# ScalarE fetches 64 columns of x a group in place of 60, VectorE 32 in place of 36, and the batch statistics of the ring stand ahead of the scores

## The chip, the cores and the metric

The kernel runs on one core of a Trainium2 chip. The metric is device time in microseconds for one execution. The core has five engines with an instruction stream each: TensorE (PE in the profile, its weight loads PEld), VectorE (DVE), ScalarE (ACT), GpSimd (POOL) and SyncE (SP). They run side by side and wait for one another on semaphores; SP and POOL issue nearly all of the DMAs here.

## The reference

One graph-attention layer with a residual, a batch normalization, a second residual and a layer normalization, all in float32. x has 12500 nodes of 128 features. There are 212500 edges, sorted by their target `dst`, each with a 128-feature `edge_attr`. Cut to what matters:

```python
Q, K, V = x @ WQ, x @ WK, x @ WV              # per node, 8 heads of 16
Eh = edge_attr @ WE                           # per edge
score = K[src] * Q[dst] / sqrt(16) * Eh
score = exp(clip(score.sum(-1), -5, 5))       # one number per edge and head
wV = segment_sum(V[src] * score, dst)
Z  = segment_sum(score, dst)
h = x + wV / (Z + 1e-6)
gnn = batchnorm(h, over the nodes) * gamma + beta
out = layernorm(x + gnn)
```

## The kernel before, in words

Edges are packed 128 to a tile, 1661 tiles in all. Four tiles that share a window of 64 target nodes form a unit, two units a group: 8 tiles, 1024 edges, 208 groups (the last one has 5 tiles). In the first 100 us or so the kernel loads x transposed into SBUF (`hx`, 128 features x 12500 nodes, resident for the whole run) and writes a table `kvd` with K and V of each node to HBM. Then it goes over the groups.

For every tile the K and V rows of its 128 source nodes have to come into a slot in SBUF. A slot holds the 8 tiles of one group, and there are nine slots. Three ways lead into it:

- **By an indirect DMA** from `kvd`, which GpSimd issues (`gather`, line 303), one for each tile. This is the common way.
- **By columns of x.** The eighth tile of most groups is not gathered. Instead ScalarE (`fetch_cols`, line 409) or VectorE (`fetch_v`, line 395) copies 128 columns of `hx`, one source node each, into a 128x128 tile (`xc` or `xv`), one instruction to a column. TensorE multiplies the full tile by the K and V weights (`cols_mm`), and ScalarE copies the product into the slot (`cols_out`, line 451). The position of a column is a register value, loaded in batches of at most 12 by a TENSOR_LOAD (`load_cols` and `load_v`, both through line 373) from the id tables `col_ids` and `v_ids`. ScalarE fetches COLS columns in a group, VectorE V_COLS, from group 8 on until the lists are used up.
- **By rows**: SP copies the rows of `kvd` one at a time (line 427), 16 in a group, and ScalarE puts them into the slot (line 437).

Functions `col_plan`, `row_plan` and `v_plan` choose at build time which groups take their eighth tile in one of the last two ways: 91 groups by ScalarE's columns, 55 by VectorE's, 24 by rows, 170 in all. The other groups gather all 8 tiles.

What one group does, by engine: TensorE makes Eh (`ps_e`, line 812) and Q per edge by a one-hot matrix (`ps_q`, line 821). VectorE multiplies both into the K part of the slot (`products`, line 837, four instructions), sums by head (`scores`, line 844), clips (line 853), makes the one-hot matrices (lines 778 and 785), finishes the attention of an earlier group (lines 889 to 896) and forms the messages (line 859). ScalarE takes the exponentials (lines 854 and 855) between the clip and the message. TensorE sums the messages by target (`gather_sum`, line 880). ScalarE copies windows and sums about (lines 766, 799, 885) and writes the new rows h into a ring of 1024 columns in SBUF (`x_out`, lines 925 and 926).

When a chunk of 512 columns of the ring is complete, `bn_parts` does two things for it: VectorE takes its mean and variance (`bn_part`, BN_STATS, line 929), and SP stores the chunk to `hT` in HBM (line 550) and then fills the place with the chunk of x that comes two later (`fill_ring`, line 546). There are 23 such refills. A refill waits for the store and for the statistics, and the `x_out` that writes into the refilled place waits for the refill.

The order on every engine is the order in which the loop at the end of the function is written (manual schedule). A gather is put into GpSimd's stream when a slot comes free after `message`; `pace` ties each gather to a VectorE or ScalarE step of the current group, so that it isn't issued earlier than that step. Behind the groups come the last statistics, the second residual and the layer normalization.

Of the kernel before, what the change touches and what calls it, by code (L numbers as in the profile page):

```python
# [33 lines left out]
RING = 1024  # L34
MARGIN = 64
PAD = 2 * MARGIN + WN
COLS = 60
LOAD = 12
V_LOAD = 12
ROOM = 16  # L40
PITCH = 80
FIRST_COL = 8
COL_LAG = 3
EXP_AT = 2
# [2 lines left out]
FIRST_ROW = 8  # L47
ROW_LAG = 2
NSEM = 6
V_COLS = 36  # L50
V_PITCH = 48
HX = 18688
RX = 80480


LAST = [3, 2]
# [23 lines left out]
def wraps(low, high):  # L80
    return high + WN > (low // RING + 1) * RING


def col_plan(sizes):
    full = sizes.count(U) // 2
    groups, end = [], P
    while FIRST_COL + -(-end // COLS) - 1 + COL_LAG < full:
        groups.append(max(NX, FIRST_COL + -(-end // COLS) - 1 + COL_LAG))
        end += P
# [4 lines left out]
def row_plan(sizes):  # L94
    full, used = sizes.count(U) // 2, set(col_plan(sizes))
    groups, end = [], P
    while True:
        g = FIRST_ROW + -(-end // SP_ROWS) + ROW_LAG
        while g in used:
            g += 1  # L100
        if g >= full:
            return groups
        used.add(g)
        groups.append(g)
        end += P


def v_plan(sizes):
    full, used = sizes.count(U) // 2, set(col_plan(sizes) + row_plan(sizes))
    tiles, at, end = [], [], P  # L110
    while True:
        m = FIRST_COL + -(-end // V_COLS)
        while (m - FIRST_COL) * COLS % P < COLS:
            m += 1
# [16 lines left out]
def gnn_kernel(  # L131
# [84 lines left out]
    nc.sync.dma_start(w_kv[:, P:], wv)  # L216
    col_ids = consts.tile([P, 2 * PITCH], I32, name="col_ids")
    v_ids = consts.tile([P, 2 * V_PITCH], I32, name="v_ids")
# [110 lines left out]
    tot = len(col_tiles) * P  # L329
    assert -(-tot // (2 * COLS)) <= P and LOAD <= ROOM and V_LOAD <= ROOM  # L330
    row_tiles = row_plan(usizes)
# [26 lines left out]
    def load_col_ids():  # L358
        load_ids(col_ids, COLS, 0, tot, LOAD)
        load_ids(row_ids, SP_ROWS, tot, tot_rows)  # L360
        load_ids(v_ids, V_COLS, tot + tot_rows, tot_v, V_LOAD)

    def addresses():
        nc.vector.tensor_scalar(row_ids, row_ids, 8 * P, None, op0=OP.mult)
        for ids in (col_ids, v_ids):
            nc.vector.tensor_scalar(ids, ids, 4, HX, op0=OP.mult, op1=OP.add)

    def whole_words(at, start, last):
        return at.with_bounds(min_val=start, max_val=start + 4 * last, guaranteed_mod_val=0, out_of_modulus=4)

    def load_at(engine, ids, q, pitch, k, n, of):
        at, n = q % 2 * pitch + k * ROOM, min(of, n - k * of)
        _, offs = nc.values_load_multi_w_load_instructions(  # L373
            ids[q // 2:q // 2 + 1, at:at + n], engines=(engine,), min_val=HX,
            max_val=HX + 4 * (N - 1), skip_runtime_bounds_check_because="node ids")
        return [o.with_bounds(min_val=HX, max_val=HX + 4 * (N - 1), guaranteed_mod_val=0, out_of_modulus=4)
                for o in offs]

    def column(at):
        return hx8[:, ds(at - HX, 4)].bitcast(F32)  # L380

    OFFV = {}

    def load_v(g, k):
        q = g - FIRST_COL
        if 0 <= q < -(-tot_v // V_COLS):
            OFFV[g, k] = load_at(ET.DVE, v_ids, q, V_PITCH, k, V_COLS, V_LOAD)

    def fetch_v(g, k, a=0, n=V_LOAD):
        offs = OFFV.get((g, k), ())[a:a + n]  # L390
        for r, off in zip(range((g - FIRST_COL) * V_COLS + k * V_LOAD + a, tot_v), offs):
            t = r // P
            if t not in XV:
                XV[t] = wp.tile([P, P], F32, name="xv", bufs=2)
            nc.vector.tensor_copy(XV[t][:, r % P:r % P + 1], column(off))  # L395
# [3 lines left out]
    def load_cols(g, k):  # L399
        q = g - FIRST_COL  # L400
        if 0 <= q < -(-tot // COLS):
            OFFS[g, k] = load_at(ET.Activation, col_ids, q, PITCH, k, COLS, LOAD)

# [149 lines left out]
    def locate_ring():  # L553
# [11 lines left out]
        nc.vector.tensor_tensor(ring_i, at, by, op=OP.subtract)  # L565
        nc.vector.tensor_scalar(ring_i, ring_i, 4, RX, op0=OP.mult, op1=OP.add)
        nc.vector.tensor_tensor(at, at, base_f[0:1, :], op=OP.not_equal)
# [3 lines left out]
    def locate():  # L571


        nc.vector.tensor_copy(base_f, base_i)
        nc.vector.tensor_scalar(base_at, base_i[0:1, :], 4, HX, op0=OP.mult, op1=OP.add)
        nc.vector.tensor_sub(lim[:, :NW - 1], base_f[:, 1:], base_f[:, :NW - 1])
# [333 lines left out]
    def x_out(g):  # L910
        if g not in AT_RING:
            n = 2 if g % 2 == 0 and g + 1 < NG else 1
            _, at = nc.values_load_multi_w_load_instructions(
                ring_i[0:1, 2 * g:2 * (g + n)], engines=(ET.Activation,), min_val=RX,
                max_val=RX + 4 * (2 * PAD + RING - WN), skip_runtime_bounds_check_because="clipped")
            at = [whole_words(a, RX, 2 * PAD + RING - WN) for a in at]
            for k in range(n):
                AT_RING[g + k] = at[2 * k:2 * k + 2]
        for h in (0, 1):
            w, at, new = 2 * g + h, AT_RING[g][h], NEW[g][:, h * WN:(h + 1) * WN]  # L920
            if wraps(low[w], high[w]):
                at = whole_words(nc.s_assert_within(at, RX, RX + 4 * (2 * PAD - WN),
                                                    skip_runtime_bounds_check_because="clipped"),
                                 RX, 2 * PAD - WN)
                nc.scalar.activation(ring8[:, 4 * RING:][:, ds(at - RX, 4 * WN)].bitcast(F32), new, AF.Copy)
            nc.scalar.activation(ring8[:, ds(at - RX, 4 * WN)].bitcast(F32), new, AF.Copy)  # L926

    def bn_part(j):
        nc.vector.bn_stats(stats[:, j, :], in_ring(cuts[j], cuts[j + 1] - cuts[j]))
        done.add(j)  # L930
# [87 lines left out]
    def bn_parts(a, b):  # L1018
        for w in range(a, b):
            for j in due.get(w, []):  # L1020
                bn_part(j)
                keep_h(j)
# [31 lines left out]
    for g in range(NG - 2):  # L1054
        within(load_rel, g + 3)
        if (g + 6) % RQ == 0 and (g + 6) // RQ in quads:
            load_quad((g + 6) // RQ)
        fetch_rows(g)
        if g % 2:
            load((g - 1) // 2 + 2)  # L1060
        within(products, g)
        load_v(g, 2)
        fetch_v(g, 0, 0, 2)
        within(scores, g)
        load_v(g, 1)
        fetch_v(g, 0, 2, 2)
        for k in range(EXP_AT):
            fetch_cols(g, k)
            load_cols(g, k + 1)
        within(clip_exp, g)  # L1070
        within(turned_onehot, g + 2)
        if g >= 2:
            denom(g - 2)
            fetch_v(g, 0, 4, 4)
            recip(g - 2)
            fetch_v(g, 0, 8, 4)
            attn(g - 2)
        fetch_v(g, 1)
        bn_parts(2 * g - 9, 2 * g - 7)
        place_step(store_places)  # L1080
        late_x = g + 1 < nxg and g + 1 not in SLOT
        if late_x:
            turn_x(g + 1, 0, True)
            turn_x(g + 1, 4, True)
            project_main(g + 1)
        within(eh_mm, g + 1)
        within(qe_mm, g + 1)
        cols_mm(g)
        paced = g >= LATE + 4
        if not paced:  # L1090
            issue()
        else:
            issue(G)
        within(onehot, g + 1)
        if paced:
            for step in (SENT[g - 1], PARTS[g][0], PARTS[g][1], PARTS[g][2], PARTS[g][4], BY["at", g - 2],
                         BY["one", g + 1], BY["exp", g]):
                pace(step)
        within(message, g)
        load_v(g + 1, 0)  # L1100
        for k in range(EXP_AT, -(-COLS // LOAD)):
            fetch_cols(g, k)
            if (k + 1) * LOAD < COLS:
                load_cols(g, k + 1)
            else:
                load_cols(g + 1, 0)
            if k == WINDOW_AT:
                within(q_window, g + 4)
        cols_out(g)
        rows_out(g)  # L1110
        fetch_v(g, 2)
        within(add_x, g - 3)
        within(q_mm, g + 3)
        within(gather_sum, g - 1)
        within(x_out, g - 3)
        within(q_out, g + 3)
        within(sums_out, g - 1)
        if g == 2:
            load_last()
            addresses()  # L1120
        if g % (RUN // 2) == 2 and g > 2 and (g // (RUN // 2) + 1) * SEC < T:
            load_section(g // (RUN // 2) + 1)
        for i, r in enumerate(runs):
            if i and g == placed[i]:
                place(r, placing)
        place_step(turn_places)
        within_checks(g)
        while free and todo and todo[0] in done and not pending:
            load_x()
        if g == NG - 3:  # L1130
            assert done >= set(range(NPRE))
            norm_first()
        if g == LATE - 1:
            tps.close()
            late.append(tps.enter_context(tc.tile_pool(name="late", bufs=1)))
        if g == LATE - 2:
            free.append(NSLOT)
            load_kv()
    last = NG - 1
    g = last - 1  # L1140
# [337 lines left out]
```

## Time and profile before

| what | value |
|---|---|
| median of 3 runs | 1971.6 us (1966.8 to 1976.07) |
| profiled execution, its own time | 1971.08 us |
| its span in the trace | 1969.3 us |
| VectorE busy | 1848.2 us, 94% |
| PE busy, weight loads | 1555.6 us (79%), 1288.4 us (65%) |
| ScalarE busy | 1532.7 us, 78% |
| GpSimd busy | 1449.3 us, 74% |
| line 395, VectorE's columns | 7040 copies |
| line 409, ScalarE's columns | 11648 copies |
| line 303, gathers from kvd | 1427 |

Busy time of an engine counts what it executes, not the loads of registers, waits and branches. A row of the page's fifth part names the line, the engine, the operation, what is written from what, the count, then busy time, the mean of one in nanoseconds and the idle time just before, with what ended it. In the timeline the start and the length of an instruction stand first, and instructions that overlap are merged with their count; on ScalarE and VectorE a short instruction begins before the one ahead of it has ended, so that the time of many is the distance of their starts and not the sum of their lengths.

### The profile page before, as it was taken

The page shows a single profiled execution, that of the slowest core. Times are in us where ns is not written, and L with a number is a line of the kernel's source. Part 1 is how long each engine was busy: PE and PEld are TensorE (multiplying, and loading weights), DVE is VectorE, ACT ScalarE, POOL GpSimd, SP SyncE. Part 2 cuts the span into 40 slices and gives each one's busy share as a digit, 9 for nine tenths or more (in the row PEclk, how much of TensorE's full clock was granted, in tenths as well). Part 3 has the DMA queues.
Part 4 walks back from the last instruction along what each step waited for, and adds up shares of the span by engine and source line. Part 5 has one row for each costly group of instructions (what it writes and reads, how often), then busy time and mean ns, then how long its engine had stood idle before and what let it go on. Part 6 is the DMA issues. An engine that isn't in the chain of part 4 may idle for free.

```text
span 1969.3 us, 64470 instructions
## 1 busy us (share of the span) xinstructions
PE 1555.6 (79%) x13025; PEld 1288.4 (65%) x13025; DVE 1848.2 (94%) x10003; ACT 1532.7 (78%) x13757; POOL 1449.3 (74%) x1527
## 2 busy tenths in 40 slices
PE   7869877778778787778778787787787877877787
PEld 6757666666666666666666666676666666666666
DVE  4458999999999999999999999999999999999997
ACT  2225888798888888888888888888898988888836
POOL 7676777777777777777777777777777777777735
PEclk9889888888898888988888888888898888888899
DMA  7854655665555656555655555655655655565553
GB/s 265 299 167 157 184 189 172 188 189 183 172 184 189 191 185 185 175 180 192 189 187 175 182 183 189 195 181 170 190 180 187 190 183 175 183 188 180 196 188 133
DMA packets 130375, 367.72 MB, mean 187 GB/s; under 512 B 37539, under 2 KB 50510, under 8 KB 116142
## 3 DMA queue, kind: packets, MB, share of 16 engines
q0 software_dynamic: 70544, 191.33, 33.1%
q1 hardware_dynamic: 56236, 171.06, 25.2%
q14 instruction: 305, 2.50, 0.4%
q8 instruction: 104, 1.70, 0.4%
q10 hardware_dynamic: 3186, 1.13, 0.3%
HBM read 337.94 MB, written 25.44 MB: 185 GB/s over the span
## 4 chain that ended last, share of the span: by engine, by line
DVE 63%; issue 10%; DVEq 9%; DMA 7%; PE 5%; ACT 3%; SPq 2%; POOL 1%; ACTq 0%; POOLq 0%
DVE xv L395 19%; DVE msg L859 10%; DVE slot L837 9%; DVEq L373 9%; DVE s L844 9%; DVE oh L778 5%; DVE ot L785 4%; DMA slot<-kvd,srcs 4%; DVE at L896 2%; DVE rz L892 1%; POOL slot L303 1%; SPq L354 1%; PE ps_e L503 1%; PE ps_q L950 1%; DVE s L853 1%
## 5 line engine op out<-in xcount | busy, mean ns | idle before, releaser
L303 POOL DMA_INDIRECT slot<-kvd,srcs x1427 | 1359.3, 953 | 449.2 <-issue 175.1
L409 ACT ACTIVATE xc<-hx 128x1 f32 x11648 | 1143.7, 192 | 31.3 <-DVE oh L778 20.9
L812 PE MATMUL ps_e<-w_e,ea 128*128 128x128 f32 x3322 | 546.7, 328 | 308.3 <-DVE slot L837 306.2
L812 PEld LDWEIGHTS ps_e<-w_e,ea 128*128 128x128 f32 x3322 | 493.2, 233 | 361.2 <-DVE slot L837 348.5
L395 DVE COPY xv<-hx 128x1 f32 x7040 | 516.2, 140 | 6.6 <-issue 5.8
L821 PE MATMUL ps_q<-qs,ot 64*128 64x128 f32 x3322 | 306.7, 323 | 4.6
L880 PE MATMUL ps_a<-msg,oh 128*64 128x136 f32 x3322 | 290.1, 296 | 1.7 <-DVE msg L859 1.7
L821 PEld LDWEIGHTS ps_q<-qs,ot 64*128 64x128 f32 x3322 | 257.8, 223 | 46.2 <-DVE slot L837 17.2
L837 DVE TENSOR_TENSOR slot<-slot,ps_e 128x512 f32<-128x512 f32 x410 | 260.9, 675 | 9.1 <-ACT xw L766 7.9
L837 DVE TENSOR_TENSOR slot<-slot,ps_q 128x512 f32<-128x512 f32 x410 | 261.1, 676 | 1.0 <-PE ps_q L821 0.7
L844 DVE TENSOR_REDUCE s<-slot 128x64 f32<-128x1024 f32 (+1 forms) x208 | 249.8, 1202 | 0.9 <-DVE xv L395 0.3
L859 DVE TENSOR_TENSOR msg<-slot,ps_m 128x1024 f32<-128x1024 f32 (+2 forms) x209 | 247.4, 1185 | 1.6 <-ACT ps_m L854 1.1
L880 PEld LDWEIGHTS ps_a<-msg,oh 128*64 128x64 f32 x3322 | 182.7, 138 | 77.7 <-issue 51.4
L926 ACT ACTIVATE ring<-ps_a 128x64 f32 x408 | 90.9, 223 | 95.5 <-DMA ring<-xT 45.6
L854 ACT ACTIVATE ps_m<-s 128x64 f32<-128x64 f32 (+1 forms) x209 | 47.6, 228 | 134.8 <-DVE s L853 128.0
L778 DVE TENSOR_TENSOR oh<-ps_i,rel 128x512 f32<-128x512 f32 x208 | 141.5, 680 | 0.0
L766 ACT ACTIVATE xw<-hx 128x64 f32 x416 | 82.7, 246 | 53.2 <-issue 38.2
L905 PE MATMUL ps_a<-ident,at 128*128 128x128 f32 x408 | 88.0, 298 | 11.0 <-ACT os L885 6.5
L785 DVE TENSOR_SCALAR ot<-rbq,wiota 128x512 f32<-128x512 uint8 x188 | 96.6, 514 | 0.0
L905 PEld LDWEIGHTS ps_a<-ident,at 128*128 128x128 f32 x408 | 74.9, 197 | 30.4 <-ACT os L885 8.6
L795 PE MATMUL ps_a<-w_q,xw 128*128 128x128 f32 x416 | 82.7, 281 | 0.4 <-ACT qs L799 0.4
L877 PE MATMUL ps_a<-msg,oh 128*1 128x136 f32 x416 | 82.0, 278 | 0.0
(191 smaller groups left out, 1535.9 us busy)
## 6 DMA issues: line engine op xcount, KB each, us to landing
ea<-eaT SPq DMA_DIRECT2D x103, 1024.0 KB
byrow<-kvd SPq DMA_DIRECT2D x3072, 1.0 KB
slot<-kvd,srcs POOLq DMA_INDIRECT x1427
rbq<-relT SPq DMA_DIRECT2D x94, 128.0 KB
kvd<-slot SPq DMA_DIRECT2D x12, 512.0 KB
kvd<-t SPq DMA_DIRECT2D x12, 512.0 KB
ring<-xT SPq DMA_DIRECT2D x24, 256.0 KB
hT<-ring SPq DMA_DIRECT2D x23, 256.0 KB
```

Of the source, the lines that this page charges most:

```text
L303: return nc.gpsimd.indirect_dma_start(out=out, out_offset=None, in_=table, in_offset=bass.IndirectOffsetOnAxis(ap=part(SRC, e, 1), axis=0))
L373: _, offs = nc.values_load_multi_w_load_instructions(ids[q // 2:q // 2 + 1, at:at + n], engines=(engine,), min_val=HX, max_val=HX + 4 * (N ...
L395: nc.vector.tensor_copy(XV[t][:, r % P:r % P + 1], column(off))
L409: nc.scalar.activation(XC[t][:, r % P:r % P + 1], column(off), AF.Copy)
L778: by(("one", g), nc.vector.tensor_tensor(one, iota_ps[:, None, :WN].to_broadcast([P, k, WN]), r[:, :, None].to_broadcast([P, k, WN]), op=O ...
L785: by(("ot", g), nc.vector.tensor_scalar(OT[g], RB[g], wiota, None, op0=OP.is_equal))
L812: by(("eh", g), nc.tensor.matmul(t[:, j - a, :], EA[g][:, j, :], w_e, start=True, stop=True))
L821: by(("qe", g), nc.tensor.matmul(QE[g][h][:, j, :], OT[g][r, j * P:(j + 1) * P], QS[g][r], start=True, stop=True))
L837: step = nc.vector.tensor_tensor(kv, kv, of[g][i][:, :b - a, :], op=OP.mult)
L844: step = nc.vector.tensor_reduce(SS[g][:, a:b, :], KV[g](a, b, 0).rearrange("p t (h d) -> p t h d", d=DH), axis=AX.X, op=OP.add)
L859: step = nc.vector.tensor_tensor(MSG[g][:, a:b, :P].rearrange("p t (h d) -> p t h d", d=DH), KV[g](a, b, P).rearrange("p t (h d) -> p t h ...
L880: by(("sum", g), nc.tensor.matmul(AGG[g][h * WN:(h + 1) * WN], OH[g][h * n + j], MSG[g][:, h * n + j, :], start=(j == 0), stop=(j == k - 1)))
```

## The change

The batch of columns that is fetched in one group moves by four from VectorE to ScalarE: COLS 60 becomes 64, V_COLS 36 becomes 32. The pitch of the id tables and the addresses of `hx` and the ring follow. The statistics of a finished chunk, with its store and refill, are asked for ahead of the scores of the group instead of behind the attention of an earlier one.

```diff
-COLS = 60
+COLS = 64
 LOAD = 12
 V_LOAD = 12
 ROOM = 16
-PITCH = 80
+PITCH = 96
...
-V_COLS = 36
+V_COLS = 32
 V_PITCH = 48
-HX = 18688
-RX = 80480
+HX = 18816
+RX = 80608
...
         within(products, g)
         load_v(g, 2)
+        bn_parts(2 * g - 9, 2 * g - 7)
         fetch_v(g, 0, 0, 2)
         within(scores, g)
...
         fetch_v(g, 1)
-        bn_parts(2 * g - 9, 2 * g - 7)
         place_step(store_places)
```

The plan follows from the sizes: 98 groups now take their eighth tile from ScalarE's columns (12544 copies), 48 from VectorE's (6144), 24 by rows: 170 again, so that the gathers from `kvd` stay 1427. ScalarE's columns run over 196 groups (194 before), VectorE's over 192 (195 before). Now 64 is not a multiple of 12, so that ScalarE has a sixth batch of 4 columns with a register load of its own.

The first place is the end of a group on ScalarE, between the window copy (`xw`) and the write into the ring. Before:

```order
L766 ACTIVATE xw<-hx 128x64 x2
L409 ACTIVATE xc<-hx 128x1 x12
L373 TENSOR_LOAD col_ids
L451 ACTIVATE slot_46705<-ps_e 128x256
L913 TENSOR_LOAD ring_i
L926 ACTIVATE ring<-ps_a 128x64 x2
```

Now:

```order
L766 ACTIVATE xw<-hx 128x64 x2
L409 ACTIVATE xc<-hx 128x1 x12
L373 TENSOR_LOAD col_ids
L409 ACTIVATE xc<-hx 128x1 x4
L373 TENSOR_LOAD col_ids
L451 ACTIVATE slot_42476<-ps_e 128x256
L913 TENSOR_LOAD ring_i
L926 ACTIVATE ring<-ps_a 128x64 x2
```

Two rows are new: a register load (of 4 values) and four copies; the load of the next group's first 12 values stands behind them.

The second place is VectorE in a group in which a chunk of the ring is complete. Before, from the last piece of the attention to the message:

```order
L896 SCALAR_TENSOR_TENSOR at<-os,keep,rz 128x128
L395 COPY xv<-hx 128x1 x12
L929 BN_STATS stats<-ring 128x6
L777 TENSOR_TENSOR oh<-rel,lim 128x1
L778 TENSOR_TENSOR oh<-ps_i,rel 128x512
L859 TENSOR_TENSOR msg<-slot_41104,ps_m 128x8x128
```

Now, from the columns at the end of the group before to the clip:

```order
L395 COPY xv<-hx 128x1 x8
L837 TENSOR_TENSOR slot_41182<-slot_41182,ps_e 128x4x128 x2
L837 TENSOR_TENSOR slot_41182<-slot_41182,ps_q 128x4x128 x2
L373 TENSOR_LOAD v_ids
L929 BN_STATS stats<-ring 128x6
L395 COPY xv<-hx 128x1 x2
L844 TENSOR_REDUCE s<-slot_41182 128x64
L373 TENSOR_LOAD v_ids
L395 COPY xv<-hx 128x1 x2
L853 TENSOR_SCALAR s<-s 128x64
```

The statistics stand between the products and the scores, and the last batch of columns in a group has 8 copies where it had 12. In this place BN_STATS waits for ScalarE's writes to the ring by a wait of its own; in the old one an earlier VectorE instruction had waited for a later ScalarE one.

The third place is SP ahead of the fourth group, where the id tables are loaded. Before:

```order
L354 DMA col_ids<-rsrc 97x2x12 x5
L354 DMA col_ids<-rsrc 1x8
L354 DMA row_ids<-rsrc 96x32
L354 DMA v_ids<-rsrc 97x2x12 x3
L354 DMA v_ids<-rsrc 1x12 x4
L354 DMA v_ids<-rsrc 1x8
```

Now:

```order
L354 DMA col_ids<-rsrc 98x2x12 x5
L354 DMA col_ids<-rsrc 98x2x4
L354 DMA row_ids<-rsrc 96x32
L354 DMA v_ids<-rsrc 96x2x12 x2
L354 DMA v_ids<-rsrc 96x2x8
```

One full list transfer more (98x2x4 in place of 1x8), and five transfers of a single row are gone.

## The prediction

> **What bounds the kernel now.** First the page's head, for the shares of the engines.
>
> ```profile
> span 1969.3 us, 64470 instructions
> PE 1555.6 (79%) x13025; PEld 1288.4 (65%) x13025; DVE 1848.2 (94%) x10003; ACT 1532.7 (78%) x13757; POOL 1449.3 (74%) x1527
> ```
>
> VectorE looks like the bound, and GpSimd like an engine with a quarter to spare. The busy times by stretch say otherwise (POOL's columns alone: stretch, length, busy time and count, clock, DMA share, GB/s).
>
> ```profile
> 300.00:500.00 200.00, 151.47 (x160) 0.89 0.59 182
> 900.00:1100.00 200.00, 151.52 (x160) 0.90 0.60 187
> 1500.00:1700.00 200.00, 151.50 (x160) 0.86 0.60 188
> ```
>
> GpSimd issues exactly 160 gathers in each 200 us, one every 1.25 us, and its timeline shows the same 0.30 us between any two. That gap is part of a gather; the only real waits are two early ones. The end of the stream is in the same view.
>
> ```profile
> 163.77 0.95 POOL L303 DMA_INDIRECT slot<-kvd,srcs  x1 [7.49 <-DVE rz L889]
> 184.99 0.94 POOL L303 DMA_INDIRECT slot<-kvd,srcs  x1 [2.71 <-DVE msg L859]
> 1876.68 0.95 POOL L303 DMA_INDIRECT slot<-kvd,srcs  x1 [0.30 <-DMA slot<-kvd,srcs]
> 1885.55 0.95 POOL L303 DMA_INDIRECT slot<-kvd,srcs  x1 [0.30 <-issue]
> 1891.79 0.95 POOL L303 DMA_INDIRECT slot<-kvd,srcs  x1 [0.30 <-issue]
> ```
>
> From 185 to 1893 us GpSimd runs without a stop. So there are two streams, gathers and groups, and the slots between them are the buffer. Which one sets the end? The last group has 5 tiles, so the last five gathers are its own; seven before them (from 1877.93 to 1885.55) belong to the group ahead, and 1876.68 closes the one before that, the third last. The chain of waits has one case in which VectorE did wait for a gather; it shows how long a gather takes to land, counted from its start.
>
> ```profile
> 173.79 2.66 DMA slot<-kvd,srcs
> ```
>
> VectorE's timeline has the products of the last three groups:
>
> ```profile
> 1900.56 1.28 DVE L837 TENSOR_TENSOR slot<-slot,ps_e 128x512 f32<-128x512 f32 x2
> 1911.42 0.68 DVE L837 TENSOR_TENSOR slot<-slot,ps_e 128x512 f32<-128x512 f32 x1
> 1917.20 0.54 DVE L837 TENSOR_TENSOR slot<-slot,ps_e 128x384 f32<-128x384 f32 x1
> ```
>
> The third last group begins at 1900.56 on rows that had landed by 1876.68 + 2.66 = 1879.34: 21.2 us of stock. The second half of the next (1911.42) has 1911.42 - 1888.21 = 23.2, the last one still more. So VectorE's side sets the end, but GpSimd stands 21 us behind it: **whatever the group loop gains beyond 21 us is lost to the gathers**, which this change leaves in number and rate.
>
> Then the groups of one engine in a long steady stretch, 300 to 1800 us, first ScalarE, then VectorE, then GpSimd:
>
> ```profile
> L409 ACT ACTIVATE xc<-hx 128x1 f32 x10290 | 1010.4, 192 | 25.3 <-DVE oh L778 17.9 <-issue 6.7
> L926 ACT ACTIVATE ring<-ps_a 128x64 f32 x344 | 76.6, 223 | 56.9 <-DMA ring<-xT 39.4 <-PE ps_a L880 6.0 <-ACT slot L451 2.5
> L854 ACT ACTIVATE ps_m<-s 128x64 f32<-128x64 f32 x172 | 39.1, 228 | 85.2 <-DVE s L853 81.6 <-DVE xv L395 1.9 <-DVE oh L778 0.5
> L889 DVE TENSOR_SCALAR rz<-os 128x8 f32<-128x8 f32 x171 | 29.5, 172 | 5.4 <-ACT os L885 5.4
> L303 POOL DMA_INDIRECT slot<-kvd,srcs x1193 | 1136.4, 953 | 363.9 <-issue 129.6 <-DVE xv L395 53.7 <-DVE slot L837 50.9
> ```
>
> 172 exponentials in 1500 us are 8.72 us a group. VectorE waits for others for about 7 us in all of it, so its own need is 8.68. ScalarE waits 17.9 + 39.4 + 6.0 + 84.0 = 147 us for others, 0.86 a group; its own need is **7.86 us**. ScalarE has room, but less than the 78% of the page make one think: 0.86 us a group.
>
> **VectorE's term.** Four copies fewer in each group from 8 to 199.
>
> ```profile
> 841.31 0.81 DVE L395 COPY xv<-hx 128x1 f32 x12
> 842.04 1.27 DVE L837 TENSOR_TENSOR slot<-slot,ps_e 128x512 f32<-128x512 f32 x2
> ```
>
> Twelve copies take 842.04 - 841.31 = 0.73 us to the start of what follows, 0.061 each. 7040 - 6144 = 896 copies are 54.7 us, 0.24 a group: 8.68 becomes 8.44. The shorter register load lies under the message and saves nothing.
>
> **ScalarE's term.** Four copies more and one register load.
>
> ```profile
> 916.27 2.33 ACT L409 ACTIVATE xc<-hx 128x1 f32 x24
> 921.34 0.40 ACT L766 ACTIVATE xw<-hx 128x64 f32 x2 [0.23 <-issue]
> 921.65 1.21 ACT L409 ACTIVATE xc<-hx 128x1 f32 x12
> 1794.10 0.40 ACT L766 ACTIVATE xw<-hx 128x64 f32 x2 [0.47 <-issue]
> L373 ACTq TENSOR_LOAD <-col_ids x971: 767/802/1977, 173.9 to 1874.7; - x195
> L758 ACTq TENSOR_LOAD <-base_at x104: 303/311/750, 36.5 to 1881.2; - x104
> ```
>
> 24 copies take 2.33 us and 12 take 1.21, so 12 more take 1.12, 0.093 each, and the load of 12 registers between the two batches (0.80 us) shows no gap: it is hidden under copies already queued. The four copies cost 0.37 us. The new load has 4 registers, as `base_at` has, and should take 0.31. What it exposes has no row; the nearest one is the window copy, ahead of which in every second group two loads follow each other: the gap is 0.23 there, 0.47 at its worst. In the new place four copies stand between the two loads and give 0.37 of cover. Bounds: 0 (all hidden, as under the batches) and 0.47. I take 0.10, nearer the hidden case, since 0.37 of new cover stands against 0.31 of new load. ScalarE's own need becomes 7.86 + 0.47 = 8.33.
>
> Its waits come on top as far as they are not for VectorE's scores: 39.4 for the ring, 17.9 for the place codes behind L778, 6.0 for PE.
>
> **The statistics' term.** They move ahead by the reduce and what follows it. One group of that kind, and SP's waits:
>
> ```profile
> 904.27 0.47 ACT L926 ACTIVATE ring<-ps_a 128x64 f32 x2
> 905.18 1.27 DVE L837 TENSOR_TENSOR slot<-slot,ps_q 128x512 f32<-128x512 f32 x2
> 910.04 0.68 DVE L929 BATCH_NORM_STATS2 stats<-ring 128x6 f32<-128x512 f32 x1
> SPq L546 <- DMA hT<-ring: 97.7, 23, 9.6
> SPq L546 <- DVE stats L929: 28.8, 11, 4.0
> ```
>
> The statistics would start behind the products at 906.4 instead of 910.0, 3.6 us earlier. SP's refill waited last for the statistics 11 times (28.8 us), and for the store 23 times (97.7 us); only the first kind gets earlier, and I take 9 of ScalarE's 39 us at the ring from it. Another 5 go because a ScalarE group that is 0.47 longer reaches the refill later. Bounds: 0 and 28.8. So 25 stay, with 14 of the 17.9 and the 6.0: 45 us in 172 groups, 0.26 each. VectorE's sum is not changed by the move: 26 instructions as before. The new wait for `x_out`, with the scores, clip, exponential and message queued behind it, finds the ring written by 904.74, 1.7 us before it is asked for. It costs something only where ScalarE runs later than that; bounds 0 and, at 0.6 us for each of 24 chunks, 14 us; I take 1.
>
> **The start's term.** The id tables, loaded while VectorE stands still:
>
> ```profile
> 102.41 12.23 SPq L354 DMA_DIRECT2D col_ids<-rsrc  x6
> 115.08 7.73 SPq L354 DMA_DIRECT2D v_ids<-rsrc  x8
> 124.55 0.38 DVE L366 TENSOR_SCALAR v_ids<-v_ids 128x96 int32<-128x96 int32 x1 [5.33 <-DMA v_ids<-rsrc]
> ```
>
> Five full lists and a single row took 12.23 us, about 2.2 a list. One more list is +2.2; of the 7.73 us of v_ids the five single rows are 7.73 - 3 x 2.2 = 1.1, which go. So +1 us (from -1.1 to +2.2), and nothing hides it: GpSimd's two waits at 163.77 and 184.99 are for VectorE's groups behind this point, so both streams start later.
>
> **The sum.** ScalarE's side is the longer of the two now: 8.33 + 0.26 = 8.59 us a group against VectorE's 8.44, and against 8.72 before. That is 0.13 in each of some 192 groups, 25 us. The gathers let 21.2 of it through. With +1 at the start, and 2 for groups that meet the gathers unevenly (a group of 8 gathers takes 10.0 us, one of 7 takes 8.8) and for the statistics' wait, 18 us remain of the profiled execution's 1971.1 us (span 1969.3 and 1.8 around it; the runs' median is 1971.6): **1953 us**.
>
> **A rule on the gathers.** With no column copies at all (110 to 150 us) and with them:
>
> ```profile
> 110.00:150.00 40.00, 30.37 (x32) 0.82 0.52 147
> 200.00:240.00 40.00, 30.43 (x32) 0.88 0.60 184
> ```
>
> 32 gathers in 40 us both times: VectorE's copies do not hold the gathers up. Were they held up by 0.061 us for each copy, 896 fewer would end the stream 55 us earlier and the loop's 25 us would come through whole: 1971 + 1 - 25 = 1947. The Trainium skill has that rule (SBUF — State Buffer, section "SBUF: two separate sides"): a float32 copy from SBUF to SBUF on VectorE locks GpSimd out of the port through which it writes descriptors. The trace does not bear it out for copies of one column, and the case gets 0.05.
>
> **Rivals.** (1) *The register loads come into the open, and ScalarE sets a slower pace.* From an exposed gap of 8.72 - 7.86 - 0.37 - 0.26 = 0.23 us a group on there is no gain left; at 0.35 each group is 0.12 longer, 23 us over 192 groups, 1995 us; at the worst gap seen, 0.47, 2017. For it: the gaps of 0.23 and 0.47 ahead of the window copy; against it: the four copies between. Chance 0.11. (The Trainium skill, DMA: Bandwidth & Descriptors, section "Latency and other measured facts", gives a register load a floor of about 0.6 us. By that the new load outlasts its cover by 0.23, estimated from that page, and the change would gain nothing; the 0.311 of the 4-register load above speaks against it.) (2) *ScalarE takes most of the gain*: an exposed gap of 0.20 leaves 0.03 a group, 6 us, 1966 us. Chance 0.21. (3) *VectorE's 54.7 us come through*: 1917 us. GpSimd's last gather at 1891.79 and ScalarE's 8.33 exclude it; I give 0.01.
>
> **How the numbers follow.** The forecast has 0.62, the freer gathers 0.05. The range holds the forecast's own, from 1947 (no unevenness, an earlier start) up into the second rival at 1968. 0.5%, 10 us, is about what a measurement of this kernel tells from no change. Faster than 1961: forecast, freer gathers, 0.04 of the second rival, 0.72 with the rest; within: 0.17 of the second rival; slower: 0.11.
>
> **What would show it.** Right: the stock ahead of the third last group's products falls from 21 us to a few, VectorE shows waits for gathers late in the run, ScalarE's wait for the scores falls from 81.6 us to a third or less, and GpSimd's last gather stays at 1893 to 1895. Wrong: if the stock is still above 15 us, ScalarE (or the new wait of the statistics) was the bound, and its gaps ahead of L451 and L926 have grown; if the last gather ends elsewhere, the rate or the start was misjudged.

## The result, and the profile after

The changed kernel takes 1952.9 us (median of 5 runs, 1951.1 to 1954.5) against 1973.1 us of the kernel before (5 runs, 1966.8 to 1976.1). The ratio is 0.9899, with a 95% interval from 0.9883 to 0.9915: about 20 us faster, clear of the noise. The profiled execution took 1951.9 us, its span is 1950.1.

The page's head, then the groups of ScalarE from 300 to 1800 us, then two of VectorE and GpSimd's gathers in the same stretch:

```profile
span 1950.1 us, 64649 instructions
PE 1548.8 (79%) x13025; PEld 1279.0 (66%) x13025; DVE 1801.1 (92%) x9107; ACT 1613.6 (83%) x14653; POOL 1454.3 (75%) x1527
```

```profile
L409 ACT ACTIVATE xc<-hx 128x1 f32 x11073 | 1085.7, 193 | 26.0 <-DVE oh L778 16.2 <-issue 7.7 <-DVE msg L859 1.1
L926 ACT ACTIVATE ring<-ps_a 128x64 f32 x346 | 77.3, 223 | 37.6 <-DMA ring<-xT 15.7 <-ACT xc L409 11.3 <-PE ps_e L812 3.6
L766 ACT ACTIVATE xw<-hx 128x64 f32 x346 | 69.7, 248 | 34.8 <-issue 34.6
L451 ACT ACTIVATE slot<-ps_e 128x256 f32<-128x256 f32 x129 | 49.6, 384 | 34.1 <-DMA slot<-kvd,srcs 16.6 <-issue 12.1 <-PE ps_e L812 4.7
L854 ACT ACTIVATE ps_m<-s 128x64 f32<-128x64 f32 x173 | 39.4, 228 | 12.1 <-DVE s L853 5.5 <-DVE xv L395 2.1 <-issue 1.7
L837 DVE TENSOR_TENSOR slot<-slot,ps_e 128x512 f32<-128x512 f32 x346 | 222.8, 681 | 17.9 <-DMA slot<-kvd,srcs 14.1 <-PE ps_e L812 2.6 <-issue 1.0
L929 DVE BATCH_NORM_STATS2 stats<-ring 128x6 f32<-128x512 f32 x21 | 14.5, 693 | 14.6 <-ACT ring L926 14.6
L303 POOL DMA_INDIRECT slot<-kvd,srcs x1191 | 1138.5, 956 | 363.3 <-issue 131.2 <-DVE xv L395 51.2 <-DVE slot L837 36.3
```

ScalarE's wait for the scores (L854 for L853) fell from 81.6 us to 5.5: ScalarE is the longer side of the loop now. VectorE has two waits that it did not have: 14.1 us for gathers, 14.6 for the ring at the statistics. The page's chain of work that ended last shows the same by line. Before:

```profile
DVE xv L395 19%; DVE msg L859 10%; DVE slot L837 9%; DVEq L373 9%; DVE s L844 9%; DVE oh L778 5%; DVE ot L785 4%; DMA slot<-kvd,srcs 4%; DVE at L896 2%; DVE rz L892 1%; POOL slot L303 1%; SPq L354 1%; PE ps_e L503 1%; PE ps_q L950 1%; DVE s L853 1%
```

Now:

```profile
DMA slot<-kvd,srcs 15%; ACT xc L409 13%; DVE xv L395 10%; DVE slot L837 7%; DVE s L844 6%; DVEq L373 4%; DVE ot L785 2%; DVE oh L778 2%; POOL slot L303 2%; DVE msg L859 2%; ACT ring L926 2%; PE ps_e L812 2%; ACTq L373 1%; DVE at L896 1%; PE ps_e L503 1%
```

Landing gathers (`slot<-kvd,srcs`) went from 4% of the span to 15%, and ScalarE's column copies, not listed before, have 13%.

Busy time by stretch shows where the bound changes; VectorE's is the third pair of columns, GpSimd's the fifth:

```profile
600.00:800.00 200.00, 159.85 (x1429) 130.70 (x1429) 199.25 (x1084) 186.26 (x1759) 151.81 (x159) 0.92 0.60 186
1000.00:1200.00 200.00, 158.61 (x1386) 130.14 (x1382) 196.61 (x1060) 182.26 (x1717) 151.55 (x159) 0.89 0.59 186
1400.00:1600.00 200.00, 159.19 (x1356) 129.12 (x1355) 190.02 (x1026) 177.09 (x1660) 151.51 (x159) 0.88 0.59 184
1600.00:1800.00 200.00, 152.34 (x1313) 125.25 (x1311) 189.89 (x1017) 177.37 (x1652) 151.52 (x160) 0.89 0.58 181
```

GpSimd issues 159 or 160 gathers in every stretch, as before. VectorE is nearly full (196.61 of 200 us) as late as 1000 to 1200 us and has some 10 us of air in 200 from 1400 on. In between, at 1280.71, it waits for a gather for the first time in the steady loop:

```profile
1280.71 0.69 DVE L837 TENSOR_TENSOR slot<-slot,ps_e 128x512 f32<-128x512 f32 x1 [1.22 <-DMA slot<-kvd,srcs]
```

There the loop has caught up with the gathers, and from there on it goes at their pace. The exponentials give the pace while stock lasts (200 to 1100 us; count, then the first and the last start). The kernel before:

```profile
L854 ACT ACTIVATE ps_m<-s x103: 221/228/229, 206.5 to 1098.6; 128x64 f32<-128x64 f32 x103
```

The changed kernel:

```profile
L854 ACT ACTIVATE ps_m<-s x105: 226/228/228, 204.9 to 1094.7; 128x64 f32<-128x64 f32 x105
```

That is 892.1 / 102 = 8.75 us a group before and 889.8 / 104 = 8.56 now. The end of both streams in the timeline, GpSimd's and VectorE's:

```profile
1875.36 0.95 POOL L303 DMA_INDIRECT slot<-kvd,srcs  x1 [0.30 <-DVE slot L837]
1890.42 0.95 POOL L303 DMA_INDIRECT slot<-kvd,srcs  x1 [0.30 <-DVE rz L892]
...
1880.87 1.28 DVE L837 TENSOR_TENSOR slot<-slot,ps_e 128x512 f32<-128x512 f32 x2
```

The third last group begins at 1880.87 on rows that had landed by 1875.36 + 2.66 = 1878.02. The stock is 2.9 us, where it was 21.2. The same sum can be made for every group, counted from 0, with the number of gathers that the plan gives each. Before, the stock shrank from 59 us at group 24 to 21 at group 205. In the changed kernel it shrinks from 55 us at group 24 to 2 at group 138 (1279 us) and never exceeds 7 us from there on. From the last gather to the end of the span it was 77.5 us before and is 59.7 now: 17.8 of the 19.2 us by which the profiled spans differ. The other 1.4 are in the gathers, whose last one starts at 1890.42 in place of 1891.79. The last five groups are not set by gathers alone: behind its last wait for one (at 1854.57) VectorE waits 5.2 us for a check of the placed codes, whose matmul (L702) had waited 4.5 us for ScalarE's sums (L885).

```profile
1866.86 0.15 DVE L703 CAST bad_i<-ps_a 1x1 int32<-1x1 f32 x1 [5.18 <-PE ps_a L702]
```

**The start.** Here the trace does not look as forecast. SP's id lists and VectorE's address step after them:

```profile
106.33 5.36 SPq L354 DMA_DIRECT2D col_ids<-rsrc  x6
112.32 1.94 SPq L354 DMA_DIRECT2D v_ids<-rsrc  x3
115.97 0.37 DVE L366 TENSOR_SCALAR v_ids<-v_ids 128x96 int32<-128x96 int32 x1 [1.87 <-DMA v_ids<-rsrc]
167.78 1.28 DVE L837 TENSOR_TENSOR slot<-slot,ps_e 128x512 f32<-128x512 f32 x2
```

A list of 98 rows takes 0.9 us, one of 96 rows 0.65; a list of 97 rows took 2.2. The steady loop starts at 167.78 us, where it started at 176.86, although the lists began 3.9 us later in this execution (106.33, where 102.41), and GpSimd's two waits at 163.77 and 184.99 are gone altogether.

### The profile page after: what moved, and what is told of

It reads as the page before. It is cut to its first block, busy times and chain, and to the rows that moved or that the text cites. A ratio compares the mean times of both kernels' runs of the same rounds, so it can differ in the third digit from the quotient of the medians.

```text
span 1950.1 us, 64649 instructions
## 1 busy us (share of the span) xinstructions
PE 1548.8 (79%) x13025; PEld 1279.0 (66%) x13025; DVE 1801.1 (92%) x9107; ACT 1613.6 (83%) x14653; POOL 1454.3 (75%) x1527
## 4 chain that ended last, share of the span: by engine, by line
DVE 34%; ACT 19%; DMA 19%; issue 11%; PE 7%; DVEq 4%; ACTq 3%; POOL 2%; SPq 0%; POOLq 0%
DMA slot<-kvd,srcs 15%; ACT xc L409 13%; DVE xv L395 10%; DVE slot L837 7%; DVE s L844 6%; DVEq L373 4%; DVE ot L785 2%; DVE oh L778 2%; POOL slot L303 2%; DVE msg L859 2%; ACT ring L926 2%; PE ps_e L812 2%; ACTq L373 1%; DVE at L896 1%; PE ps_e L503 1%
## 5 line engine op out<-in xcount | busy, mean ns | idle before, releaser
L303 POOL DMA_INDIRECT slot<-kvd,srcs x1427 | 1363.5, 956 | 439.8 <-issue 175.3
L409 ACT ACTIVATE xc<-hx 128x1 f32 x12544 | 1229.9, 193 | 32.5 <-DVE oh L778 18.9
L395 DVE COPY xv<-hx 128x1 f32 x6144 | 463.4, 144 | 0.6
L926 ACT ACTIVATE ring<-ps_a 128x64 f32 x408 | 91.2, 224 | 69.1 <-PE ps_a L880 24.1
L766 ACT ACTIVATE xw<-hx 128x64 f32 x416 | 83.4, 248 | 57.2 <-issue 39.8
L451 ACT ACTIVATE slot<-ps_e 128x256 f32<-128x256 f32 x146 | 56.1, 384 | 38.5 <-DMA slot<-kvd,srcs 18.7
```

Source lines behind the costliest of these rows:

```text
L303: return nc.gpsimd.indirect_dma_start(out=out, out_offset=None, in_=table, in_offset=bass.IndirectOffsetOnAxis(ap=part(SRC, e, 1), axis=0))
L409: nc.scalar.activation(XC[t][:, r % P:r % P + 1], column(off), AF.Copy)
```

## The experiments

Eleven of the twelve runs fell on three chips on which the kernel before takes 2866 to 2874 us, and one on a chip on which it takes 1971. What the eleven say is told apart from the one. The changed kernel itself was not run on the three.

### Columns alone

Against the changed kernel:

```diff
         load_v(g, 2)
-        bn_parts(2 * g - 9, 2 * g - 7)
         fetch_v(g, 0, 0, 2)
...
         fetch_v(g, 1)
+        bn_parts(2 * g - 9, 2 * g - 7)
```

> Columns 64 and 32 alone, the statistics in their old place, once more beside the kernel before. If the kernel before takes about 1971 us on this chip: 1953 us, within 2, if the gathers cap the gain (the prediction); up to 1962 if the move of the statistics is a part of it. If it takes some 2870 us again, with ScalarE's instructions at 0.165 us each: 2990 us, since a group then has 5 to 6 instructions more on ScalarE.

This is the run on a chip like the first. It took 1952.1 us (1951.4 to 1954.3) against 1971.3, ratio 0.9901 (0.9879 to 0.9924): the columns, with the lists that they bring, are the whole gain, and the statistics' move adds nothing to it. Its trace says why the move adds nothing; how the gain divides between the columns and the lists it does not show. The exponentials from 200 to 1100 us:

```profile
L854 ACT ACTIVATE ps_m<-s x106: 212/228/229, 201.1 to 1094.2; 128x64 f32<-128x64 f32 x106
```

From 300 to 1800 us, VectorE's products and ScalarE's writes to the ring:

```profile
L837 DVE TENSOR_TENSOR slot<-slot,ps_e 128x512 f32<-128x512 f32 x346 | 222.7, 678 | 31.5 <-DMA slot<-kvd,srcs 28.0 <-issue 3.4
...
L926 ACT ACTIVATE ring<-ps_a 128x64 f32 x346 | 77.3, 223 | 38.5 <-DMA ring<-xT 18.7 <-ACT xc L409 10.0 <-PE ps_e L812 3.1
```

And the last gather:

```profile
1886.67 0.95 POOL L303 DMA_INDIRECT slot<-kvd,srcs  x1 [0.30 <-issue]
```

With the statistics in their old place a group takes 893.1 / 105 = 8.51 us while stock lasts, 0.05 less than in the changed kernel: the move slows the loop a little, since VectorE waits for the ring. What the loop gained by that went into VectorE's wait for gathers, 28.0 us against 14.1 in the same stretch, and the time stayed. That is the cap at work: a loop that is faster by itself ends no earlier. Its first wait for a gather comes at 1186.56, about 94 us before that of the changed kernel:

```profile
1186.56 0.69 DVE L837 TENSOR_TENSOR slot<-slot,ps_e 128x512 f32<-128x512 f32 x1 [1.98 <-DMA slot<-kvd,srcs]
```

The cap is not quite hard at the very end: here the last gather is 3.8 us earlier than in the changed kernel, the third last group begins 2.2 us earlier (1878.70, where 1880.87), the last one 0.9 (1897.16, where 1898.01), and the span is only 0.3 shorter. Behind the last wait for a gather (at 1849.97) VectorE waits 5.2 us for the check of the placed codes, as it does in the changed kernel, so that ScalarE has a part in the last groups of both.

The same kernel ran on one of the other chips too:

> The changed kernel with the statistics in their old place, so columns 64 and 32 alone. If the gathers cap the gain (the prediction), whatever the place of the statistics costs lies in the stock: 1953 us, within 2. If ScalarE's loop sets the end and the move of the statistics is a part of the gain, some 9 us of ScalarE's waits at the ring come back: up to 1962 us.

On that chip it took 2991.0 us against 2872.2: ratio 1.041 (1.039 to 1.044), a loss of 4%.

### What is different on those chips

ScalarE's copies of the columns-alone kernel there, in the timeline, and the group over the whole run:

```profile
1511.85 0.39 ACT L409 ACTIVATE xc<-hx 128x1 f32 x3 [0.30 <-issue]
1512.61 0.20 ACT L409 ACTIVATE xc<-hx 128x1 f32 x1 [0.38 <-issue]
1513.34 0.20 ACT L409 ACTIVATE xc<-hx 128x1 f32 x1 [0.52 <-issue]
...
1514.79 0.20 ACT L409 ACTIVATE xc<-hx 128x1 f32 x1 [0.38 <-issue]
1515.52 0.20 ACT L409 ACTIVATE xc<-hx 128x1 f32 x1 [0.52 <-issue]
1516.23 0.20 ACT L409 ACTIVATE xc<-hx 128x1 f32 x1 [0.51 <-issue]
...
L409 ACT ACTIVATE xc<-hx 128x1 f32 x12544 | 1360.4, 193 | 713.8 <-issue 695.7 <-DMA slot<-kvd,srcs 8.4 <-DVE oh L778 2.8
```

Copies that follow each other every 0.093 us elsewhere start 0.72 us apart for stretches of several us, with nothing that the profile shows them to wait for; the whole run has 696 us of it. VectorE's copies are hardly touched:

```profile
L395 DVE COPY xv<-hx 128x1 f32 x6144 | 466.5, 145 | 11.8 <-issue 11.1
```

In the middle half of the run ScalarE starts one instruction (register loads and semaphores counted) every 0.164 to 0.166 us in the first four kernels, whatever their columns; in the changed kernel on the first chip it is 0.10. VectorE waits 897 us in the columns-alone run there for ScalarE's sums (L889 for L885). So the rate at which ScalarE starts instructions sets the pace there, not the gathers, and a change that gives ScalarE more instructions loses: 118.8 us in 192 groups is 0.62 us for four copies and a register load in each. The granted TensorE clock is lower on these chips too, 0.74 to 0.76 where the first has 0.89; whether that is a cause of the gaps or stands beside them no run separates.

> The kernel of g_after (the changed kernel, 38 gathers replaced by plain loads of 128 rows on SP, so those tiles hold other rows than the reference has), on such a chip: 1927 to 1938 us if the gathers cap the gain, since ScalarE's loop at 8.58 us a group would have ended some 25 us earlier; 1950 to 1955 us if ScalarE's loop sets the end of the changed kernel by itself.

```diff
+    def plain(out, table, e):
+        return nc.sync.dma_start(out=out, in_=table[:P, :])
...
     def pace(step):
+        while queued and queued[0][0] is plain:
+            plain(*queued.pop(0)[1:])
...
-                queued.append((gather, KV[g](j, j + 1, 0, 2 * P).rearrange("p a d -> p (a d)"), kvd,
+                queued.append((plain if j == 0 and g >= 15 and g % 5 == 0 else gather, KV[g](j, j + 1, 0, 2 * P).rearrange("p a d -> p (a d)"), kvd,
```

The rule takes groups 15, 20 and so on to 205, which are 39 and not 38: the traces have 1388 gathers. It ran three times, each time on such a chip: 2921.3, 2931.6 and 2925.6 us, ratios 1.017, 1.022 and 1.018. The two other expectations for it were:

> The changed kernel with 38 of the 1427 gathers (the first tile of every fifth group from 15 on) replaced by one plain load of 128 rows of the table, issued by SP; so those tiles hold other rows than the reference has, and all else stays. GpSimd's stream is 47 us shorter. If the gathers cap the gain (the prediction: ScalarE's own pace of 8.59 us would save 25 us, of which 21 came through; the trace after, with 8.58 us a group while stock lasts, 60 groups short of the end: some 25 us are left over), the time falls to 1927 to 1938 us. If ScalarE's loop sets the end of the changed kernel already: 1950 to 1955. On a chip on which ScalarE's instructions set the pace, no change against the changed kernel, which would be 4% above the kernel before there.

> The kernel of gathers_less once more (the changed kernel with 38 of its 1427 gathers replaced by plain loads of 128 rows on SP). On a chip on which the kernel before takes about 1971 us: the cap theory says 1927 to 1938 us, for the columns alone ran 8.53 us a group while stock lasted and met the gathers some 80 groups before the end; if ScalarE's loop sets the end, 1948 to 1955 us, with VectorE's waits for gathers gone and nothing gained. On a chip on which it takes some 2870 us: 2920 to 2930 us as twice before.

Because the gathers are not the bound there, the cap could not be tested by taking gathers away; on a chip like the first, that was not run. The expectation of the first of the three (g_after) also missed on these chips: I had said no change against some 4%, and the kernel came out 2% above the kernel before. On the same chip, 2931.6 stands against 2996.9 of the changed kernel with other lists (slow_again, below): 65 us, 1.7 us for each gather left out. ScalarE's mean step fell with it, to 0.159 us, and the gaps ahead of its column copies from 699.8 to 621.3 us. In the next kernel they are down to 613.7 us with only six gathers fewer, and that one is the slowest of all, so that what the gaps hang on the runs do not settle.

> The changed kernel with V_COLS 34 in place of 32 and SP_ROWS 18 in place of 16 (the id tables in 98, 96 and 96 rows): VectorE's columns then give 51 tiles and SP's rows 27, six gathers fewer. If the gathers set the end and the loop has 25 us to spare, 6 x 1.25 = 7.5 us less: 1945 us. VectorE's need becomes 8.44 + 0.12 = 8.56 us a group, still not above ScalarE's 8.58. If the loop has no such room, the two columns more come to light, 0.12 x 192 = 23 us: up to 1975 us; if SP falls behind with 18 rows of 0.36 us in 8.7 us, the ring's refills come later and it ends above 1953.

```diff
-SP_ROWS = 16
+SP_ROWS = 18
...
-V_COLS = 32
+V_COLS = 34
```

The list form of the lists experiment below and the addresses `HX` and `RX` go with it. 3042.8 us, ratio 1.061 (1.058 to 1.065), the slowest of all. SP's queue shows a price: 36 rows, two groups' worth, took 20.17 us here, 0.56 a row, where the changed kernel's first trace, on the faster chip, has 11.64 us for 32, 0.36 a row. First that trace, then this kernel's:

```profile
904.08 11.64 SPq L427 DMA_DIRECT2D byrow<-kvd  x32
```

```profile
1508.81 20.17 SPq L426 DMA_DIRECT2D byrow<-kvd  x36
```

SP's instructions come slower here, as ScalarE's do. The whole edit, with its 384 rows more, costs some 46 us against slow_again on the same chip; that the rows are the reason is not shown apart from the rest. Whether this version gains its 7.5 us on a chip like the first was not run; as it stands it beats neither kernel.

### The statistics alone

Against the kernel before:

```diff
         load_v(g, 2)
+        bn_parts(2 * g - 9, 2 * g - 7)
         fetch_v(g, 0, 0, 2)
...
         fetch_v(g, 1)
-        bn_parts(2 * g - 9, 2 * g - 7)
```

> The kernel before with the statistics moved ahead of the scores, columns 60 and 36 as they were. VectorE's own need (8.68 us a group) sets the pace, so less waiting of ScalarE at the ring brings nothing: 1971 us, within 2, and ScalarE's wait at the ring for DMA falls from 39.4 us to about 30. If the move carried a part of the gain by itself: 1962 us. If the new wait for the ring holds VectorE up (17 us of such waits stand in the trace after): up to 1985 us.

2873.7 against 2872.2 us, ratio 0.9995 (0.9974 to 1.0017), on one of the three chips. No effect, as in the columns-alone run, though VectorE waited 82.9 us for the ring there in 22 statistics:

```profile
DVE stats L929 <- ACT ring L926: 82.9, 22, 5.8
```

VectorE is far from the bound on that chip: its waits for ScalarE's sums (L889) are 565.7 us here and 644.8 in the kernel before with other lists (e_lists, below) on the same chip, so that the new wait stands where another one stood. On a chip like the first the statistics alone were not run; there the move's share is the difference between the changed kernel's ratio of 0.9899 and 0.9901 with the columns alone.

### The lists

Against the kernel before; the order of the three lists in the source changes with it:

```diff
-    return [2 * g for g in col_plan(sizes) + row_plan(sizes) + v_plan(sizes)[0]]
+    return [2 * g for g in col_plan(sizes) + v_plan(sizes)[0] + row_plan(sizes)]
...
-        m, rest = divmod(total, 2 * n)
-        for p, j, k, c, w in ((0, 0, m, 2, n), (m, 0, 1, 1, min(rest, n)), (m, 1, 1, 1, rest - n)):
+        for p, j, k, c, w in ((0, 0, -(-total // (2 * n)), 2, n),):
...
-        load_ids(row_ids, SP_ROWS, tot, tot_rows)
-        load_ids(v_ids, V_COLS, tot + tot_rows, tot_v, V_LOAD)
+        load_ids(row_ids, SP_ROWS, tot + tot_v, tot_rows)
+        load_ids(v_ids, V_COLS, tot, tot_v, V_LOAD)
```

> The kernel before with one edit: the tables of column ids are loaded in transfers of 98 rows each (one row more than is needed, read from what follows in the list), where it has transfers of 97 rows and single rows for the rest; columns 60 and 36 and the place of the statistics stay. As the prediction has it, a list costs about 2.2 us whatever its rows, and only the six single rows go, 1 to 2 us: 1969 to 1971 us. The rival that the trace after suggests: 97 rows is a slow form on SP (2.21 us, against 0.82 for 98 rows) and the group loop of the changed kernel starts 9 us earlier for that reason; then VectorE's loop, which sets the end here, ends 9 us earlier too: 1962 us, with GpSimd's waits of 7.5 and 2.7 us before 185 us gone.

> The kernel of e_lists once more, beside the kernel before on the same chip, because the first four runs fell on a chip on which ScalarE started one instruction in 0.165 us on the mean, whatever the kernel, and the kernel before took 2872 us. If the kernel before takes about 1971 us here: 1962 if the form of the lists is worth the 9 us by which the group loop started earlier in the changed kernel; 1969 to 1971 if it is worth nothing beyond the single rows, as the prediction has it. If ScalarE's instructions set the pace here too, the lists bring nothing that can be measured.

> The kernel of e_lists (the kernel before with its id tables loaded in 98 rows each, columns 60 and 36), on a chip on which the kernel before takes about 1971 us: 1962 us if the form of the lists is worth the 9 us by which the changed kernel's group loop starts earlier, since VectorE's loop sets the end here; 1969 to 1971 us if it is worth no more than the single rows, as the prediction has it.

Three times on such chips: ratios 0.9976 (0.9951 to 1.0001), 0.9983 (0.9959 to 1.0008) and 0.9995 (0.9972 to 1.0018). Each interval includes no change; the medians lie 2 to 8 us below the kernel before. The opposite edit splits off the last row of each list of the changed kernel:

```diff
-        for p, j, k, c, w in ((0, 0, m, 2, n), (m, 0, 1, 1, min(rest, n)), (m, 1, 1, 1, rest - n)):
+        assert not rest
+        o = m if to is row_ids else m - 1
+        for p, j, k, c, w in ((0, 0, o, 2, n), (o, 0, m - o, 2, n)):
```

> The changed kernel with each table of column ids loaded in 97 (VectorE's: 95) rows and the last row by itself. If 97 rows is the slow form, the group loop starts later by 6 x 1.4 us and nine single rows of 0.45 us, 12 us, and by 5 more if 95 is slow too; GpSimd then waits for free slots for that long early in the run, nothing later makes it up since the gathers run back to back to the end: 1963 to 1969 us. If the form of the lists has nothing to do with it, only the single rows: 1953 to 1957 us.

> The kernel of e_slow (the changed kernel with each id table loaded in 97 or 95 rows and a last row by itself), on such a chip: the group loop starts 12 to 17 us later. If GpSimd then waits as long for free slots, and nothing makes it up, 1963 to 1969 us; if the stream of gathers has slack early in the run, less comes through; if the form of the lists has nothing to do with it, 1953 to 1957 us.

2999.3 us (1.044, 1.041 to 1.046) and 2996.9 us (1.043, 1.040 to 1.047), beside 1.041 of the columns alone. So on the total the lists do nothing that can be measured there. On SP's own time the form of a list does what the first traces show. The column lists of the statistics-alone kernel (five of 97 rows and a single row), then those of e_lists (five of 98 rows), least, median and longest in ns:

```profile
L354 SPq DMA_DIRECT2D col_ids<-rsrc x6: 785/1941/2611, 120.3 to 129.5; - x6
```

```profile
L353 SPq DMA_DIRECT2D col_ids<-rsrc x5: 817/846/1001, 123.6 to 127.4; - x5
```

The same columns, one row more: 0.85 us in place of 1.94 on the median. The opposite edit agrees: the column lists take SP 16.73 us in e_slow (six of 97 rows and six single rows) and 5.52 with the columns alone (six of 98 rows) on the same chip. That part is shown by edits to the lists alone. What it is worth in the total on a chip like the first is read from the traces alone.

## Why the prediction was right, and where not

1953 us was forecast and 1952.9 measured. The steps did not all hold, and that the number fits so closely is luck.

**The cap: right. The loop: right, with too small a gain.** The stock fell from 21.2 to 2.9 us, and VectorE waits for gathers late in the run. While stock lasted, the loop's pace came out at 8.56 us a group (8.59 forecast), but the kernel before took 8.75 in the same stretch: the gain was 0.19 a group where I had 0.13. Half of that difference is the pace, half the stretch, in which the kernel before goes a little slower than the 8.72 that I took. At 0.19 the loop had some 36 us to give in 192 groups, far more than the stock. ScalarE's own need: its waits for others in the rows above, 16.2 + 1.1 + 15.7 + 3.6 + 16.6 + 4.7 + 5.5 + 2.1 = 65.5 us, leave (1500 - 65.5) / 173 = 8.29 us a group, against 8.33. In the same terms the kernel before had 7.83 (the prediction's 7.86 left out 5.0 us at L451), so that the growth is 0.46, where 0.47 was forecast. The four copies are as costed: 16 take 1.58 us, where 12 took 1.21.

**The extra register load: about as taken.** ScalarE's gaps of its own ahead of L409, L451 and L766 grew from 6.7 + 4.5 + 33.7 to 7.7 + 12.1 + 34.6 us, by 9.5 in 173 groups. The rows before, in the same stretch:

```profile
L766 ACT ACTIVATE xw<-hx 128x64 f32 x342 | 68.2, 246 | 33.7 <-issue 33.7
L451 ACT ACTIVATE slot<-ps_e 128x256 f32<-128x256 f32 x129 | 49.5, 383 | 16.4 <-DMA slot<-kvd,srcs 5.0 <-issue 4.5 <-PE ps_a L880 0.2
```

The gaps ahead of the ring's writes (L926 and L925), in which ScalarE waits for nothing but its own copies just before, grew as well, from 2.5 + 1.8 + 1.7 + 1.6 to 11.3 + 0.8 + 4.8 + 0.6 us, by 9.9. Before, in the view of waits for the one and in the rows for the other:

```profile
ACT ring L926 <- ACT xc L409: 1.8, 6, 0.6
L925 ACT ACTIVATE ring<-ps_a 128x64 f32 x71 | 15.9, 224 | 5.5 <-ACT xc L409 1.7 <-ACT slot L451 1.6 <-PE ps_a L880 0.7
```

Now:

```profile
L925 ACT ACTIVATE ring<-ps_a 128x64 f32 x70 | 15.6, 223 | 6.7 <-ACT xc L409 4.8 <-PE ps_e L812 0.8 <-ACT slot L451 0.6
```

Together that is 0.11 a group, where I took 0.10 between bounds of 0 and 0.47. That the new load is what these gaps wait for is read from their place, not shown by a run. The upper bound was misread: 0.47 is not the worst gap ahead of the window copy, the same trace has one of 0.80.

```profile
1430.03 0.40 ACT L766 ACTIVATE xw<-hx 128x64 f32 x2 [0.80 <-issue]
```

The load of 4 registers takes 0.31 us at the least:

```profile
L373 ACTq TENSOR_LOAD <-col_ids x1176: 304/793/1860, 164.8 to 1874.0; - x196
```

(The Trainium skill, DMA: Bandwidth & Descriptors, section "Latency and other measured facts", has a floor of about 0.6 us for a register load. This trace does not agree: by that floor nothing would have been gained.)

**The statistics: mis-sized twice.** I gave the move 9 us of ScalarE's ring waits and the longer group 5. The waits fell from 39.4 to 15.7 us, but with the statistics in their old place to 18.7: at most 3 are the move's, and 20.7 came with the columns and their lists. And the new wait of the statistics for the ring, taken as 1 us in all, is 14.6 us in the stretch and 17 in the run: ScalarE, now the longer side, writes the ring later than VectorE asks for it. The slack of 1.7 us was read from a trace in which ScalarE was ahead. The cap hid the loss, 0.05 us a group against the columns alone.

**The start: wrong sign.** "One more list is +2.2, five single rows go, so +1 us" took 2.2 us as the price of a list. It was the price of 97 rows. With 98 and 96 rows the lists took 8 us where they took 20, and the loop started 9.1 us earlier. The row that I quoted said "x6" and "x8" and not how many rows; the order of the instructions did, and I used it only to count.

**The last gather: 1890.4, not 1893 to 1895.** GpSimd's early waits, 7.5 and 2.7 us, 9.6 above the usual gap, are gone with that start. Against them stand a first gather from `kvd` 3.9 us later in this execution, and gathers that are each 3 ns longer (953 and 956 ns on the mean in the rows at L303), 4 us over 1427 of them. In the columns-alone kernel, whose first one starts at 88.76 as it did before (88.92), the last one starts at 1886.67, 5.1 us earlier than before.

The first gather before, after, and with the columns alone:

```profile
88.92 0.95 POOL L303 DMA_INDIRECT slot<-kvd,srcs  x1 [4.64 <-issue]
```

```profile
92.83 0.94 POOL L303 DMA_INDIRECT slot<-kvd,srcs  x1 [4.79 <-issue]
```

```profile
88.76 0.94 POOL L303 DMA_INDIRECT slot<-kvd,srcs  x1 [4.75 <-issue]
```

So the number is met by luck: some 10 us that the start gave to the gathers, unforeseen, against some 8 that took them back, as unforeseen. With lists as slow as before, GpSimd's waits would have stayed, and the end would lie near 1960: 1890.4 + 9.6 for the last gather, 59.7 from there to the end and 1.8 around the span are 1961.5, or 1957.6 if the 3.9 us of the late first gather vanish in those waits. By that estimate the faster lists are worth 6 to 10 of the 20 us; it is worked out and not run on such a chip.

**The rivals.** ScalarE did not take most of the gain, nor did the loads come into the open. The freer gathers fell with the sign turned round: 896 copies fewer on VectorE, and a gather became longer by 3 ns, not shorter by any part of 0.061 us a copy. (The rule of the Trainium skill, SBUF — State Buffer, section "SBUF: two separate sides", is not borne out for copies of one column, by this trace as by the one before.) What no rival had is a chip on which the rate of ScalarE's instructions is the bound: there the columns alone cost 4%, in the direction of the first rival and for another reason.

## What to carry to other kernels

When two engines feed one loop, write down how far the second one stands behind the first: here 21 us of stock said what a 25 us saving could bring, and a loop that got faster still brought nothing more. A term read from one row belongs to that row's shape and to who was ahead in that trace: the price of a list was that of 97 rows, and the slack at the ring that of a ScalarE with time to spare. And a kernel tuned so that two engines end together moves its bound with the chip: time it on more than one before work is shifted to the engine with the most instructions.

## What was not expected of the hardware

- A list transfer of 97 rows holds SP for 1.9 to 2.2 us on the median, one of 98 rows for 0.7 to 0.9, one of 96 rows for 0.6 to 0.7, with at most 24 values of 4 bytes a row.
- On three of four chips that ran the experiments, ScalarE's and SP's instructions start 0.7 us apart for stretches, while VectorE's copies are hardly touched (145 ns on the mean, 11 us of gaps in the whole run); the kernel before takes 2870 us there and 1971 on the fourth. With 39 gathers replaced by plain loads the gaps were fewer and the time 65 us shorter. What causes them is open.
- A gather takes 953 ns on the mean before and 956 in both kernels with fewer copies on VectorE. Over all the traces the mean is 947 to 956 ns, in no order that follows the loop's pace (956 at some 13 us a group with the statistics alone), so what the 3 ns come from is open.
